# Third and fourth token group of a transformer block: x loaded by channels, its mean and scale sent through DRAM, in place of TensorE transposes

## The chip, the cores and the metric

The kernel runs on one core of a Trainium2 chip. A core has TensorE (in the profile PE for matmuls and PEld for the loads of weights), VectorE (DVE), ScalarE (ACT), GpSimd (POOL), and SyncE (SP), which here only issues transfers; 16 DMA engines move data between DRAM and the on-chip SBUF. Matmuls write to PSUM, of which the kernel holds eight banks of 128x512 numbers. Each engine works through its own instructions in order and waits by semaphores for the others. The metric is the device time of one execution in microseconds (us); the median of several runs counts.

## The reference

One transformer block over x, 2048 tokens of 1024 channels, all in 32-bit floats:

```python
x = x + _layernorm(attn(_layernorm(x), Wqkv, bqkv, Wo, bo))
x = x + _layernorm(ffn(_layernorm(x), W_gate, W_up, W_down))
# _layernorm(x) = (x - mean) / sqrt(var + 1e-5) over the channels
# attn: qkv = x @ Wqkv + bqkv, one head of 256; softmax(q k^T / 16) v; then @ Wo + bo
# ffn:  (silu(x @ W_gate.T) * (x @ W_up.T)) @ W_down.T, inner size 2752
```

The change touches the first `_layernorm(x)` and the form in which its result reaches the product with Wqkv.

## The kernel before

Each 32-bit factor of a matmul is kept as two parts, hi (a rounded copy, written by ScalarE) and lo (the source less hi, written by VectorE). The helper `split` (lines 108 to 110) makes both; line 109 is the copy, line 110 the subtraction. A product is then three matmuls (`mm3`, lines 140 to 144: hi hi, hi lo, lo hi) for each block of 128 channels.

A matmul contracts over the partitions, so the normalised x must lie with channels on the partitions: `xT[g]`, eight channel blocks x (hi, lo) x 512 tokens, for a group g of 512 tokens. There are four groups (NG = 4), each of four token tiles (TB = 4) of 128 tokens. `xT` has two buffers, used in turn: a tile of its own for groups 0 and 2, and `a2` for groups 1 and 3, so that the profile names the latter's writes "a". The rows of x come as token tiles, 128 tokens x 1024 channels, into four buffers `xin` = `f4[0:4]` (`load_x`, line 160, by SP's queue). For each tile:

- `norm_stats` (lines 112 to 122): two bn_stats over 512 channels (line 116), an aggregate (119) and the addition of epsilon (120) on VectorE, then the power -1/2 on GpSimd (121). Results are one mean and one scale per token, each a [128, 1] column of a small tile.
- the normalisation in place (line 127 in `norm_rows`; in the first two groups line 240 or 294 or, on ScalarE, 245).
- eight transposes of 128x128 on TensorE into two PSUM banks (line 135 in `transpose_rows`; line 251 in the first two groups), and hi and lo from the banks into `xT` (lines 109 and 110; 218 and 221 in the first two groups).

Groups 0 and 1 are prepared by code written out by hand (lines 292 to 354 and 467 to 482). Groups 2 and 3 are prepared in the loop of lines 483 to 490: in round g (1 to 3), step i of four calls `prep1((g + 1) * TB + i, ...)` (lines 164 to 170) for one token tile of the next group, and then `qk(g, i, ...)`, the i-th of four output blocks (k in two, q in two) of group g, 24 matmuls over the eight channel blocks into bank 4 or 5. After `prep1`, the buffer is loaded with the tile four further on. Then come the four `v_block(g, tb)`, 16 matmuls each into bank 6 or 7, one per token tile; such a block needs the eight channel blocks of its own 128 tokens alone. Drains of the banks: k by line 178 (ScalarE) and 179 (VectorE), q of groups 1 to 3 by line 182 and a store to DRAM (`q_d`, line 183), v by lines 193 to 195 with `split`. After the loop, `scores(0, j)` (lines 377 to 384; k of group j with q of group 0, six matmuls into bank j), the first softmax, and attention over 16 query tiles; then the gate, up and down products, which take most of the time.

The order of each engine's instructions is set by a scheduler that runs when the kernel is built and goes by priority (the order of the program) and by its own estimate of when data are ready. So PE's matmuls of one block can be mixed with those of another whose data are there. An instruction in `pin(...)` or with `tc.keep_in_program_order` stays behind the one traced just before it on its engine. The bn_stats of the loop are pinned in this way; line 127, the transposes of line 135, `split`, `qk` in the loop and `v_block` aren't.

Buffers that the change uses: `f2p[1]` and `f4[4]` (128 x 1024 each) hold raw weights in the first stage. After that `f4[4]` takes the q of the next group for attention (`q_load`, line 370, split by lines 374 and 375), `f4[0]` and `f4[1]` the rows of wo (line 512, on ScalarE's queue), and `f2p[1]`, `f4[1]` and `f4[3]` rows of x for the residual (line 1143).

Of the kernel before, what the change touches and what calls it, by code (L numbers as in the profile page):

```python
# [8 lines left out]
F32 = mybir.dt.float32  # L9
F32R = mybir.dt.float32r  # L10
AF = mybir.ActivationFunctionType
ALU = mybir.AluOpType
# [3 lines left out]
P = 128  # L16
T = 2048
C = 1024
D = 256
F = 2752  # L20
NT = T // P
NC_ = C // P
G = 512
NG = T // G
TB = G // P
# [6 lines left out]


@with_exitstack
def block_kernel(ctx, tc, x, wqk, wv, bqk, bv, wo, bo, wgu, wlast, wd, out):

# [9 lines left out]
    nc = tc.nc  # L48
# [4 lines left out]
    def tl(p, shape, dt, name):  # L53
        return p.tile(shape, dt, tag=name, name=name, bufs=1)
# [3 lines left out]
    ident = tl(cpool, [P, P], F32, "ident")  # L58
# [13 lines left out]
    def small_tile():  # L72
        small_n[0] += 1
        return small[small_n[0] % NSM]

    bank_pool = pool("banks", space=PSUM)
    bank = [tl(bank_pool, [P, 512], F32, f"bank{i}") for i in range(8)]

    dram = ctx.enter_context(tc.tile_pool(name="dram", bufs=1, space=bass.MemoryType.DRAM))
    q_d = [tl(dram, [P, 2, G], F32, f"q_d{g}") for g in range(NG)]  # L80
    xT_d = [tl(dram, [C, G], F32, f"xT_d{g}") for g in range(NG)]
    at_d = [tl(dram, [P, C], F32, f"at_d{t}") for t in range(NT)]
    x1_d = [tl(dram, [P, C], F32, f"x1_d{t}") for t in range(NT)]
# [10 lines left out]
    f4 = [tl(cpool, [P, C], F32, f"f4_{i}") for i in range(5)]  # L94
    f2p = [tl(cpool, [P, C], F32, f"f2p{i}") for i in range(2)]
# [9 lines left out]
    def f32(ap):  # L105
        return ap.bitcast(F32)

    def split(hi, lo, src, lo_engine=None):
        nc.scalar.copy(hi, src)  # L109
        (lo_engine or nc.vector).tensor_tensor(lo, src, f32(hi), ALU.subtract)  # L110

    def norm_stats(halves, pin=None):

        s = small_tile()
        for i, h in enumerate(halves):
            b = nc.vector.bn_stats(s[:, 6 * i : 6 * i + 6], h)
            if pin:
                pin(b)
        nc.vector.bn_aggr(s[:, 12:14], s[:, 0:12])
        nc.vector.tensor_scalar(s[:, 14:15], s[:, 13:14], EPS, None, ALU.add)  # L120
        nc.gpsimd.tensor_tensor(s[:, 15:16], s[:, 14:15], mhalf, ALU.pow)
        return s[:, 12:13], s[:, 15:16], s

    def norm_rows(t, pin):

        m, r, _ = norm_stats([t[:, 0:512], t[:, 512:1024]], pin)
        nc.vector.tensor_scalar(t, t, m, r, ALU.subtract, ALU.mult)

    def transpose_rows(t, dst, tb, banks):

        for hf in range(2):
            b = banks[hf]
            for j in range(4):
                cb = 4 * hf + j
                nc.tensor.transpose(b[:, j * P : (j + 1) * P], t[:, cb * P : (cb + 1) * P], ident)  # L135
            src = b.rearrange("p (j t) -> p j t", j=4)
            cols = slice(tb * P, (tb + 1) * P)
            split(dst[:, 4 * hf : 4 * hf + 4, 0, cols], dst[:, 4 * hf : 4 * hf + 4, 1, cols], src)

    def mm3(o, w, m, first, last, pin=lambda i: i):  # L140

        pin(nc.tensor.matmul(o, w[0], m[0], start=first, stop=False))  # L142
        pin(nc.tensor.matmul(o, w[0], m[1], start=False, stop=False))  # L143
        return pin(nc.tensor.matmul(o, w[1], m[0], start=False, stop=last))  # L144
# [6 lines left out]
    xin, wraw, qst = f4[0:4], [f4[4], f2p[1]], f2[0:2]  # L151
# [5 lines left out]
    xT = [tl(x0_pool, [P, 8, 2, G], F32R, "xT0"), a2]  # L157

    def load_x(t):
        nc.sync.dma_start(xin[t % TB], x[t * P : (t + 1) * P, :])  # L160

    WARM = 34

    def prep1(t, banks):

        r = xin[t % TB]
        norm_rows(r, tc.keep_in_program_order)
        transpose_rows(r, xT[(t // TB) % 2], t % TB, banks)
        if t + TB < NT:
            load_x(t + TB)  # L170

    def qk(g, i, b, pin=lambda i: i):
        xg = xT[g % 2]
        for c in range(8):
            mm3(b, (wqk_s[i][:, c, 0, :], wqk_s[i][:, c, 1, :]), (xg[:, c, 0, :], xg[:, c, 1, :]), c == 0, c == 7, pin)
        if i < 2 or g == 0:
            dst = kT(i, g) if i < 2 else qa[:, i - 2, :, :]
            pin(nc.scalar.activation(dst[:, 0, :], b, AF.Identity, bias=bqk_s[:, i : i + 1]))
            pin(nc.vector.scalar_tensor_tensor(dst[:, 1, :], b, bqk_s[:, i : i + 1], f32(dst[:, 0, :]), ALU.add, ALU.subtract))
        else:  # L180
            s = qst[i % 2]
            nc.scalar.activation(s, b, AF.Identity, bias=bqk_s[:, i : i + 1])
            nc.sync.dma_start(q_d[g][:, i - 2, :], s)

    def v_block(g, tb, b):
        xg = xT[g % 2]
        cols = slice(tb * P, (tb + 1) * P)
        for c in range(8):
            nc.tensor.matmul(b, xg[:, c, 0, cols], wv_s[:, c, :, :].rearrange("p a f -> p (a f)"), start=(c == 0), stop=False)  # L189
            nc.tensor.matmul(b[:, D:], xg[:, c, 1, cols], wv_s[:, c, 0, :], start=False, stop=(c == 7))  # L190
        k = g * TB + tb
        s = vst[tb % 2]
        nc.vector.tensor_tensor(s, b[:, :D], bv_s, ALU.add)
        nc.vector.tensor_tensor(s, b[:, D:], s, ALU.add)
        split(vt[:, k, 0, :], vt[:, k, 1, :], s)
# [4 lines left out]
    pin = tc.keep_in_program_order  # L200
# [33 lines left out]
    def stats(tb):  # L234
        r = xin[tb % TB]
        return norm_stats([r[:, L], r[:, R]], pin)
# [55 lines left out]
    m, r, _ = stats(0)  # L292
# [190 lines left out]
    for g in range(1, NG):  # L483
        for i in range(4):
            if g + 1 < NG:
                prep1((g + 1) * TB + i, (bank[2 * (i % 2)], bank[2 * (i % 2) + 1]))
            qk(g, i, bank[4 + i % 2])
        if 0 < g < NG - 1:
            for tb in range(TB):
                v_block(g, tb, bank[6 + tb % 2])  # L490
# [86 lines left out]
    pin = tc.keep_in_program_order  # L577
# [72 lines left out]
    class Slot:  # L650
        t = None
# [465 lines left out]
    for i in range(NT):  # L1117
# [40 lines left out]
        cb = i - EARLY - 3  # L1158
# [129 lines left out]
```

## Time and profile before

| what | value |
|---|---|
| median of 3 runs (lowest, highest) | 1676.95 us (1676.39, 1677.01) |
| profiled execution | 1676.83 us |
| its span in the trace | 1675.0 us |
| granted TensorE clock | 0.999 |
| DMA moved | 271.02 MB, mean 162 GB/s |

The span is the time from the first to the last instruction in the trace; 1.83 us of the profiled execution lie around it. An engine's busy time is the sum of its instructions' records. Matmuls are pipelined, so the record of one (386 ns for 512 columns) overlaps the next, and the distance between two starts is what one costs. "The chain" is the sequence of instructions and waits followed back from the last instruction: what isn't on it could be shorter at no effect. Views by line name the line of the kernel that issued an instruction; "a<-bank" means that tile a is written from a tile bank, buffer numbers left out. Transfers are listed by issue, with the time from the issue to the landing of the data.

### The profile page before, as it was taken

The numbers are of one execution on the slowest core, as the hardware profiler recorded it, in microseconds if no ns is written. First come the engines' busy times: TensorE is split into PE (matmuls) and PEld (weight loads), VectorE is DVE, ScalarE is ACT, GpSimd is POOL, SyncE is SP. The second block draws the span as 40 slices with busy tenths as digits, with TensorE's granted clock in tenths as the row PEclk, the third lists the DMA queues.
The fourth block names the chain that finished last, engine by engine and source line by source line (L and its number), as shares of the span: only waits on it lengthen the run. The fifth ranks groups of instructions, "written<-read, shape, count | busy, mean of one in ns | idle before, by whom it ended". The sixth has DMA issues, their size and how long they took to land.

```text
span 1675.0 us, 21258 instructions
## 1 busy us (share of the span) xinstructions
PE 1664.4 (99%) x7850; PEld 1391.1 (83%) x7850; DVE 1101.3 (66%) x1679; ACT 698.3 (42%) x1043; POOL 91.9 (5%) x121
## 2 busy tenths in 40 slices
PE   9999999999999999999999999999999999999998
PEld 8888888888888888888888888888888888888887
DVE  7553676767877777677578457965555665465458
ACT  4222455544634444444365444433333333354342
POOL 1000010000011111111000000100000000000001
PEclk9999999999999999999999999999999999999999
DMA  6221023335656666666468656533322223586653
GB/s 217 83 80 41 12 101 114 113 128 186 221 173 220 215 211 229 220 218 205 158 226 260 199 186 213 198 115 125 113 101 95 95 95 126 214 267 194 199 185 123
DMA packets 131160, 271.02 MB, mean 162 GB/s; under 512 B 13296, under 2 KB 30064, under 8 KB 131056
## 3 DMA queue, kind: packets, MB, share of 16 engines
q1 hardware_dynamic: 129616, 266.65, 47.7%
q10 hardware_dynamic: 1440, 3.02, 0.5%
q8 instruction: 61, 1.00, 0.3%
q14 instruction: 43, 0.35, 0.1%
HBM read 185.73 MB, written 83.89 MB: 161 GB/s over the span
## 4 chain that ended last, share of the span: by engine, by line
PE 96%; DVE 2%; DMA 1%; issue 0%; ACT 0%; POOL 0%; SPq 0%; POOLq 0%; DVEq 0%; ACTq 0%
PE bank L782 71%; PE bank L144 4%; PE bank L142 4%; PE bank L143 4%; PE bank L417 3%; PE bank L418 2%; PE bank L401 2%; PE bank L189 1%; PE bank L190 1%; PE bank L521 1%; PE bank L274 0%; PE bank L135 0%; DMA f<-x 0%; PE bank L968 0%; DMA out<-bo_s 0%
## 5 line engine op out<-in xcount | busy, mean ns | idle before, releaser
L782 PE MATMUL bank<-a 128*128 128x512 f32 (+1 forms) x960 | 226.4, 386 | 0.0
L782 PE MATMUL bank<-xb,a 128*128 128x512 f32 x912 | 212.5, 389 | 0.2 <-DVE a L110 0.2
L782 PEld LDWEIGHTS bank<-a 128*128 128x128 f32 x960 | 179.0, 188 | 36.6
L782 PEld LDWEIGHTS bank<-xb,a 128*128 128x128 f32 x912 | 170.9, 188 | 36.0 <-DVE a L110 0.6
L109 ACT CAST a<-f2p 128x1024 fp32r<-128x1024 f32 (+2 forms) x123 | 107.0, 870 | 115.1 <-PE bank L782 88.2
L110 DVE TENSOR_TENSOR a<-f2p,a 128x1024 fp32r<-128x1024 f32 (+2 forms) x123 | 122.4, 995 | 44.4 <-ACT a L109 40.4
L110 DVE TENSOR_TENSOR a<-f,a 128x1024 fp32r<-128x1024 f32 (+2 forms) x82 | 83.6, 1020 | 103.3 <-ACT a L109 101.3
L782 PE MATMUL bank<-kx,a 128*128 128x512 f32 x612 | 146.0, 389 | 0.0
L782 PE MATMUL bank<-a,a 128*128 128x512 f32 x588 | 139.7, 389 | 0.0
L782 PEld LDWEIGHTS bank<-kx,a 128*128 128x128 f32 x612 | 114.9, 188 | 23.8
L782 PEld LDWEIGHTS bank<-a,a 128*128 128x128 f32 x588 | 110.3, 188 | 23.0
L782 PE MATMUL bank<-wvo 128*128 128x512 f32 (+1 forms) x498 | 120.9, 386 | 0.0
L796 DVE TENSOR_TENSOR p_s<-bank,p_s 128x512 f32<-128x512 f32 x96 | 65.2, 682 | 81.7 <-PE bank L782 45.8
L109 ACT CAST a<-f 128x1024 fp32r<-128x1024 f32 (+2 forms) x82 | 62.6, 764 | 120.0 <-PE bank L782 98.6
L782 PEld LDWEIGHTS bank<-wvo 128*128 128x128 f32 x498 | 92.9, 188 | 18.9
L782 PE MATMUL bank<-a,wvo 128*128 128x512 f32 x444 | 106.0, 389 | 0.0
L782 PE MATMUL bank<-kx,wvo 128*128 128x512 f32 x420 | 100.1, 389 | 0.0
L782 PEld LDWEIGHTS bank<-a,wvo 128*128 128x128 f32 x444 | 83.3, 188 | 17.3
L782 PEld LDWEIGHTS bank<-kx,wvo 128*128 128x128 f32 x420 | 78.8, 188 | 16.4
L110 DVE TENSOR_TENSOR wvo<-f,wvo 128x1024 fp32r<-128x1024 f32 (+1 forms) x49 | 57.1, 1166 | 50.5 <-ACT wvo L109 50.5
L417 PE MATMUL bank<-a,a 128*128 128x512 f32 x240 | 89.4, 404 | 0.9 <-ACT f2p L523 0.6
L782 PE MATMUL bank<-kx 128*128 128x512 f32 (+1 forms) x339 | 78.5, 387 | 0.0
(285 smaller groups left out, 2908.4 us busy)
## 6 DMA issues: line engine op xcount, KB each, us to landing
f2p<-wgu SPq DMA_DIRECT2D x41, 512.0 KB, 5.4
f<-x SPq DMA_DIRECT2D x30, 512.0 KB, 3.8
hd_S<-p_s SPq DMA_DIRECT2D x60, 256.0 KB, 4.5
f<-wgu SPq DMA_DIRECT2D x22, 512.0 KB, 3.5
wr<-wgu SPq DMA_DIRECT2D x21, 512.0 KB, 5.6
f<-wd SPq DMA_DIRECT2D x20, 512.0 KB, 5.0
hd_A<-xi SPq DMA_DIRECT2D x40, 256.0 KB, 2.0
td_T<-f SPq DMA_DIRECT2D x40, 256.0 KB, 4.5
```

What stands on the lines that cost most here:

```text
L109: nc.scalar.copy(hi, src)
L110: (lo_engine or nc.vector).tensor_tensor(lo, src, f32(hi), ALU.subtract)
L142: pin(nc.tensor.matmul(o, w[0], m[0], start=first, stop=False))
L143: pin(nc.tensor.matmul(o, w[0], m[1], start=False, stop=False))
L144: return pin(nc.tensor.matmul(o, w[1], m[0], start=False, stop=last))
L189: nc.tensor.matmul(b, xg[:, c, 0, cols], wv_s[:, c, :, :].rearrange("p a f -> p (a f)"), start=(c == 0), stop=False)
L190: nc.tensor.matmul(b[:, D:], xg[:, c, 1, cols], wv_s[:, c, 0, :], start=False, stop=(c == 7))
L401: nc.tensor.transpose(b[:, n * P : (n + 1) * P], p_s[:, k * P : (k + 1) * P], ident)
L417: nc.tensor.matmul(b, p[:, k, 0, :], vt[:, k, :, :].rearrange("p h d -> p (h d)"), start=(k == 0), stop=False)
L418: nc.tensor.matmul(b[:, D:], p[:, k, 1, :], vt[:, k, 0, :], start=False, stop=(k == NKB - 1))
L782: one = nc.tensor.matmul(o, w[i], m[j], start=first and n == 0, stop=last and n == 2, skip_group_check=chained)
L796: nc.vector.tensor_tensor(o, a, b, op)
```

## The change

Groups 2 and 3 are prepared another way. A second input `xt` holds x of the last 1024 tokens transposed, as [2 groups, 1024 channels, 512 tokens], arranged on the host. In the first step of a round, the statistics of all four token tiles of the next group are taken from the rows, as before (`row_stats`). Mean and scale, eight [128, 1] columns, are stored to a DRAM tensor `mr_d` of [2, 512] by eight transfers; one transfer reads it back to all 128 partitions (`mr`, 1024 numbers per partition, 512 KB in all). Then four transfers load `xt` over the rows in the same four buffers, two channel blocks x 512 tokens in each (`load_columns`). In each of the four steps, `columns` subtracts the mean and multiplies by the scale, both with a different value for each column, repeated over the two channel blocks, and splits the result into `xT`. Then the buffer is loaded with the rows of the next group. The transposes of line 135, the banks 0 to 3 in the loop and the normalisation of line 127 are gone. Line numbers in the diff are those of its own.

```diff
@@ -78,6 +78,7 @@
     q_d = [tl(dram, [P, 2, G], F32, f"q_d{g}") for g in range(NG)]
+    mr_d = [tl(dram, [2, G], F32, f"mr_d{g}") for g in range(NG)]
@@ -161,13 +146,32 @@
-    def prep1(t, banks):
-
+    mr = {2: f2p[1], 3: f4[4]}
+
+    def row_stats(t):
         r = xin[t % TB]
-        norm_rows(r, tc.keep_in_program_order)
-        transpose_rows(r, xT[(t // TB) % 2], t % TB, banks)
-        if t + TB < NT:
-            load_x(t + TB)
+        m, rs, _ = norm_stats([r[:, 0:512], r[:, 512:1024]], tc.keep_in_program_order)
+        cols = slice((t % TB) * P, (t % TB + 1) * P)
+        for k, v in enumerate((m, rs)):
+            nc.sync.dma_start(mr_d[t // TB][k : k + 1, cols].rearrange("k p -> p k"), v)
+
+    def load_columns(g):
+        nc.sync.dma_start(mr[g].rearrange("p (k t) -> p k t", k=2), mr_d[g].partition_broadcast(P))
+        for n, r in enumerate(xin):
+            nc.sync.dma_start(r.rearrange("p (c t) -> p c t", c=2), xt[g - 2].rearrange("(n c p) t -> n p c t", c=2, p=P)[n])
+
+    def columns(g, n):
+
+        r = xin[n].rearrange("p (c t) -> p c t", c=2)
+        for k, op in enumerate((ALU.subtract, ALU.mult)):
+            v = mr[g][:, k * G : (k + 1) * G].unsqueeze(1).broadcast_to([P, 2, G])
+            nc.vector.tensor_tensor(r, r, v, op)
+        d = xT[g % 2][:, 2 * n : 2 * n + 2, :, :]
+        split(d[:, :, 0, :], d[:, :, 1, :], r)
+        if g + 1 < NG:
+            load_x((g + 1) * TB + n)
@@ -483,7 +487,11 @@
             if g + 1 < NG:
-                prep1((g + 1) * TB + i, (bank[2 * (i % 2)], bank[2 * (i % 2) + 1]))
+                if i == 0:
+                    for tb in range(TB):
+                        row_stats((g + 1) * TB + tb)
+                    load_columns(g + 1)
+                columns(g + 1, i)
             qk(g, i, bank[4 + i % 2])
@@ -1267,6 +1275,7 @@
+        "xt": x.reshape(2, 2 * G, C)[1].reshape(2, G, C).transpose(0, 2, 1),
```

Left out of the diff: the removal of `norm_rows` and `transpose_rows`, which nothing calls any more, and the parameter `xt` of the kernel.

## The prediction

> **What bounds the kernel now.** I read the busy shares first, then the chain that ended last, then the two stages that the change touches. On the page:
>
> ```profile
> span 1675.0 us, 21258 instructions
> PE 1664.4 (99%) x7850; PEld 1391.1 (83%) x7850; DVE 1101.3 (66%) x1679; ACT 698.3 (42%) x1043; POOL 91.9 (5%) x121
> ...
> PE 96%; DVE 2%; DMA 1%; issue 0%; ACT 0%; POOL 0%; SPq 0%; POOLq 0%; DVEq 0%; ACTq 0%
> ```
>
> TensorE is busy for 99% of the span and makes up 96% of the chain: time goes only where PE instructions go or where PE is made to wait. The changed loop (lines 483 to 490) runs from 56.85 us, when the first matmul of group 1 (counted from 0) starts, to about 131 us; group 2's first q/k matmul starts at 92.74 us. The view by stretches of time for its two rounds (columns: PE, PEld, DVE, ACT, POOL busy, granted clock, DMA share, GB/s):
>
> ```profile
> 56.85:92.74 35.89, 35.89 (x189) 30.55 (x188) 21.96 (x45) 8.97 (x16) 2.74 (x5) 1.00 0.27 88
> 92.74:130.90 38.16, 38.16 (x197) 32.19 (x196) 20.11 (x39) 9.12 (x16) 1.64 (x3) 1.00 0.25 84
> ```
>
> PE has no gap at a clock of 1.00. DVE is 61% and 53% busy, DMA a quarter: there is room beside PE, but not without end.
>
> **What is removed.** Eight token tiles with eight transposes each, 64 PE instructions. The chain view of 60 to 100 us prices a tile's eight:
>
> ```profile
> 66.22 0.87 PE bank L135 x8
> 71.68 0.87 PE bank L135 x8
> 79.38 0.87 PE bank L135 x8
> 88.90 0.87 PE bank L135 x8
> 97.48 0.87 PE bank L135 x8
> ```
>
> They stand on the chain, with matmuls directly before and after: 8 x 0.87 = **7.0 us**. (Their records sum to 8.28 us, because records overlap by the pipeline; the chain's figure is what the next matmul waits.) Per tile DVE loses one normalisation and two subtractions from PSUM, ACT two copies from PSUM. Rows: normalisation 0.81, subtractions 1.29 for the two, copies 1.07 for the two.
>
> **What is added.** Per channel tile: two 128x1024 tensor_tensor on DVE and one subtraction of that size, one ACT copy of 128x1024. The SBUF rows of that size say 1.22 us for DVE (line 221 at 28.02 us; neighbours follow after 1.14), 1.05 for ACT. A mean repeated over a middle dimension as second operand isn't in the trace; that row is the nearest and I take it, with the 0.81 us of the one-operand normalisation as the lower and 1.29 us as the upper end. DVE per tile: 3 x 1.14 = 3.4 us against 0.73 + 1.20 = 1.93 before; so +1.5 per tile, +6 per group. DVE goes to about 28 us in a round of PE that shrinks to some 33: 85%. ACT stays as it is. This is hidden as long as the order of arrival allows; so I follow the chain of each group.
>
> Group 2. The statistics now come in one block behind the last drain of group 0:
>
> ```profile
> 57.77 0.75 DVE L179 SCALAR_TENSOR_TENSOR qa<-bank,bqk_s,qa 128x512 fp32r<-128x512 f32 x1 [4.67 <-ACT qa L178]
> 58.44 1.28 DVE L116 BATCH_NORM_STATS2 small<-f 128x6 f32<-128x512 f32 x2
> 59.75 0.21 DVE L119 BATCH_NORM_AGGREGATE small<-small 128x2 f32<-128x12 f32 x1
> 60.00 0.15 DVE L120 TENSOR_SCALAR small<-small 128x1 f32<-128x1 f32 x1
> ```
>
> 58.44 to 60.15 is 1.71 us a tile, four end at 65.3; all four x tiles were issued by 51.6 us, and bn_stats is pinned behind the DVE instruction traced before it, which here is the previous tile's line 120. POOL's power (0.55) ends at 65.9. Then eight stores of [128,1] go by SP's queue, 0.33 us of issue each (up to 0.48, the row of bqk_s); six are out before, in a stretch where that queue has no other issue until 67 us. Store, wait and load by DRAM exist for q:
>
> ```profile
> 82.83 0.33 SPq L183 DMA_DIRECT2D q_d<-f2p  x1
> 85.68 0.33 SPq L370 DMA_DIRECT2D f<-q_d  x1
> ```
>
> 2.85 us from a store's issue to that of its reader, which SP had waited for. The mean/scale load is 512 KB, like the x loads of 4.2 us (list of DMA issues, below). So 66.0 + 2.85 + 4.1 = **73 us**. Bounds for both from that list (KB each, us to landing):
>
> ```profile
> f<-x SPq DMA_DIRECT2D x17, 512.0 KB, 4.2
> ...
> q_d<-f2p SPq DMA_DIRECT2D x4, 256.0 KB, 2.0
> ...
> f2p<-x SPq DMA_DIRECT2D x1, 512.0 KB, 3.4
> ...
> bo_s<-bo SPq DMA_DIRECT2D x1, 512.0 KB, 9.6
> ...
> bqk_s<-bqk SPq DMA_DIRECT2D x1, 2.0 KB, 9.0
> ```
>
> The small pieces of bqk_s (16 bytes in each partition) and the broadcast bo_s took 9.0 and 9.6 us, but at 4 to 5 us of the span, behind some 3 MB of loads. At 73 us only the four column loads (2 MB) stand in the queues, free to go from 60 us as each tile's statistics have read it. So I take the uncrowded rows and keep 12 us of lateness (9.0 + 0.3 + 9.6 against 2.85 + 4.1) as the upper end per group; the lower end is 1 us early.
>
> First pair of channel blocks: 73 + 2 x 1.14 + 1.05 + 1.2 = 77.5. The others follow by 3.4, with 3.2 us of other DVE work between (one k drain 0.75, two v blocks of 1.25): the last at **91 us**. PE: v_block of group 2 starts at 86.27 behind three tiles' transposes, so group 1's own work would end at 86.27 - 3 x 0.87 = 83.7. Then PE has scores(0,0) and scores(0,1) (banks 0 and 1 are now free): 12 matmuls of 0.228, 2.7 us. Each ready pair gives qk of two banks, 12 x 0.228, and two v blocks' share, 4 x 0.35: 4.1 us against 3.4 that DVE needs for the next. Pairs 0 to 2 (77.5, 81, 87) carry PE to 83.7 + 2.7 + 12.3 = 98.7, beyond 91. If the matmuls go in a stricter order (one qk alone, 1.37 us per pair), pair 3 is wanted at 83.7 + 2.7 + 4.1 = 90.5: at most 1, without the scores 3 us late. What goes away here is v_block of group 2 as a filler: by token tiles two of its blocks ran before group 2's tiles were complete; by channels all wait for the last pair.
>
> Group 3. load_x of tile 12 + n must now wait until pair n is split, the last at 91, landing at 95; statistics end at 96.7, POOL 97.3, store and reader 100.2, landing 104.2, pairs at 109, 112, 116 and, with the drains, 122. PE's own work of group 2 (96 x 0.228 + 64 x 0.176 = 33.1) ends at 83.7 + 33.1 = 116.8, three score blocks fill to 120.9, pairs 0 to 2 are there. Nothing to 1 us. SP issues eight stores, one load and four column loads more per group (13 x 0.33 = 4.3 us of 33); behind them wait q's stores, whose buffers are wanted a round later. The q load into f4[4] and wo's loads into f4[0], f4[1] slip by some 30 and 15 us: in the trace of before q_split runs at 123 and wo's splits at 162, later than their new landings at about 126 or close to it, and q of group 1 is wanted four attention tiles on.
>
> Sum: 1676.83 (the profiled execution: span 1675.0 and 1.83 around it) - 7.0 + stall of 0 to 3.3, of which I take 0.5 = 1670.3; the median of the runs is 0.1 above the profiled one: **1670.4**.
>
> **Two rules against the change.** The Trainium skill, "DMA: Bandwidth & Descriptors", "Rules for kernel authors", wants many small transfers made one large, since under 64 KB one pays mostly overhead, and its "Specifications" see a read-modify-write below 512 bytes; the 16 stores here move 4 bytes per partition. Its fixed part of about 2.0 us ("Anatomy of one DMA", for the GpSimd path) would, as an estimate, be 16 us if eight were paid in turn, and the sum would be like that of the slower rival. No run here yet shows such a store.
>
> **Rivals.** (1) *The new chain is late by some microseconds.* For it: DVE at 85% and in order, four transfers in line where none was. Against: PE's fillers, and that no PE wait between 25 and 131 us shows in before. Stall 3.3 to 10, time 1673.6 to 1680.3, say 1676: no difference. (2) *Slower: DRAM round trips that take the place of the transposes.* Each us by which store and broadcast land later than 73 moves pair 3 of group 2, and group 3 twice, as its x loads hang on group 2's pairs. With strict order the stall is about e in group 2 and e - 3 in group 3 for a lateness e: 2e - 3, so break-even at e = 5, slower by over 0.2% from e = 6.7. At the upper end, e = 12: 21 us, +14, 1691; with interleaved matmuls about 12.5, 1682; say 1686. For it only the crowded rows speak. (3) *It doesn't do what it says*, PE's 7 us return as waits in the softmax stage: before has only 1.4 us of PE idle from 160 to 300 us, and nothing there loses slack; up to 1676.8.
>
> **Chances and range.** Forecast (up to 1673.5) 0.62, all faster. Rivals 1 and 3: 0.18, same, which here means within 0.2% (3.35 us), about what a measurement of this kernel can tell from no change. Rival 2: 0.20, slower. Low end: 7.0 plus the 1.4 of idle gone, 1668.5. High end: to leave out at most 2 in 10 it takes in rivals 1 and 3 and part of rival 2: 1684. The forecast's own range is 1669.8 to 1673.5.
>
> **What would show it.** Right: no line 135; PE busy down by about 8 us of records; PE gapless from 57 to 120; the mean/scale load landing near 73 us, its store taking 2 to 3; group 2's first q/k matmul by 87. Wrong: PE waiting on DVE's xT near 84 to 95 or 117 to 130, stores of 5 us and more, DVE held at the first subtraction of the mean, drains of lines 179 or 193 behind it.

## The result, and the profile after

The changed kernel took 1704.22 us (median of 6 runs, 1698.78 to 1706.46) against 1676.98 for the kernel before: a ratio of 1.016, with a 95% interval of 1.0145 to 1.0175. It is slower by 27 us; the prediction had 1670.4, at most 1684. The profiled execution took 1705.52 us, 28.7 more than that of before.

The page of the changed kernel, span, busy times and the chain by engine:

```profile
span 1703.4 us, 21178 instructions
PE 1661.0 (98%) x7786; PEld 1385.9 (81%) x7786; DVE 1110.6 (65%) x1679; ACT 698.0 (41%) x1035; POOL 92.1 (5%) x121
...
PE 92%; DMA 4%; DVE 2%; issue 1%; ACT 0%; POOL 0%; POOLq 0%; DVEq 0%; SPq 0%
```

The 64 transposes are gone (7850 - 7786), and PE has less to do than before. But 4% of the chain are now transfers. The view by stretches of time of the changed kernel says where:

```profile
56.85:92.74 35.89, 26.95 (x125) 22.18 (x123) 11.03 (x22) 2.76 (x4) 2.20 (x4) 0.92 0.58 80
92.74:131.00 38.26, 31.29 (x137) 25.67 (x137) 21.27 (x35) 7.55 (x10) 2.20 (x4) 0.90 0.59 131
131.00:170.00 39.00, 23.97 (x101) 19.83 (x102) 22.17 (x29) 8.51 (x12) 0.00 (x0) 0.74 0.35 108
```

PE, full before, is idle for 9, 7 and 15 us, at a granted clock of 0.92, 0.90 and 0.74. In the first stretch the DMA engines are busy for 58% of the time and move only 80 GB/s; before it was 27% for 88. The waits of PE from 55 to 180 us are two, one ahead of each group (us in total, times, longest; line 127 is the first matmul of a q/k product in the changed kernel):

```profile
PE bank L127 <- ACT a L110: 17.7, 1, 17.7
PE bank L127 <- ACT xT L110: 13.2, 1, 13.2
```

What the hi copies of line 110 waited for, in the chain of 55 to 180 us (start, us, what):

```profile
61.40 12.20 DMA f<-xt
...
73.67 11.89 DMA mr_d<-small
...
85.60 4.47 DMA f2p<-mr_d
...
90.09 4.70 DVE f L170 x5
```

The last small store (`mr_d<-small`) was issued at 73.67, because SP had first waited for the load of an xt tile to land, from which the store needs nothing (why, is said under "Stores alone"); it took 11.9 us more until the load of mean and scale could be issued. That load took 4.5, near the predicted 4.1. SP's timeline shows the pause ahead of the last stores:

```profile
64.14 1.20 SPq L158 DMA_DIRECT2D mr_d<-small  x2
70.39 0.38 SPq L163 DMA_DIRECT2D f<-xt  x1
70.86 3.12 SPq L158 DMA_DIRECT2D mr_d<-small  x2
85.60 0.32 SPq L161 DMA_DIRECT2D f2p<-mr_d  x1
```

The list of DMA issues (KB each, us to landing) shows that both the 512-byte stores and the 512 KB loads beside them were slow:

```profile
f<-xt SPq DMA_DIRECT2D x8, 512.0 KB, 13.2
...
mr_d<-small SPq DMA_DIRECT2D x16, 0.5 KB, 13.1
```

The waits are 30.9 us. PE's timeline around the first one:

```profile
83.52 0.28 PE L194 MATMUL bank<-wvo,a 128*128 128x256 f32 x1
97.04 0.80 PE L127 MATMUL bank<-xT,wqk 128*128 128x512 f32 x1 [13.24 <-ACT xT L110]
97.63 0.63 PE L127 MATMUL bank<-kx,qa 128*128 128x512 f32 x1
```

The clock fell to half during each wait and stayed there for a while after it: from 97.04 to 100.49 us and from 146.03 to 151.64 us the trace has 8 and 13 matmul distances of which most are 0.43 us, in place of 0.23; that is 3.45 - 1.84 and 5.61 - 2.99, together an estimated 4.2 us. -7.0 + 30.9 + 4.2 = 28.1 of the 28.7.

### The profile page after: what moved, and what is told of

Its sections match the earlier page's. It is cut to its first block, busy times and chain, and to the rows that moved or that the text cites. A ratio compares the mean times of both kernels' runs of the same rounds, so it can differ in the third digit from the quotient of the medians.

```text
span 1703.4 us, 21178 instructions
## 1 busy us (share of the span) xinstructions
PE 1661.0 (98%) x7786; PEld 1385.9 (81%) x7786; DVE 1110.6 (65%) x1679; ACT 698.0 (41%) x1035; POOL 92.1 (5%) x121
## 4 chain that ended last, share of the span: by engine, by line
PE 92%; DMA 4%; DVE 2%; issue 1%; ACT 0%; POOL 0%; POOLq 0%; DVEq 0%; SPq 0%
PE bank L790 71%; PE bank L127 3%; PE bank L128 3%; PE bank L129 3%; PE bank L421 3%; DMA f<-xt 2%; PE bank L422 2%; PE bank L405 2%; DMA mr_d<-small 1%; PE bank L193 1%; DVE f L170 1%; PE bank L529 1%; DMA f<-x 1%; DVE small L117 1%; PE bank L194 0%
## 5 line engine op out<-in xcount | busy, mean ns | idle before, releaser
L111 DVE TENSOR_TENSOR a<-f,a 128x1024 fp32r<-128x1024 f32 (+2 forms) x86 | 88.3, 1028 | 106.5 <-ACT a L110 104.2
L110 ACT CAST a<-f 128x1024 fp32r<-128x1024 f32 (+2 forms) x86 | 66.7, 776 | 152.2 <-PE bank L790 99.1
```

## The experiments

Theory A: stores in pieces of 4 bytes are slow by themselves and hold up what shares the DMA engines. Rival B: they are slow only because the xt loads stand in the same queues. Rival C: SP's queue can have only so many transfers under way. Each profile below is that of one execution.

**No wait for the stores.** Mean and scale come from a row of x; the stores still run.

```diff
-        nc.sync.dma_start(mr[g].rearrange("p (k t) -> p k t", k=2), mr_d[g].partition_broadcast(P))
+        nc.sync.dma_start(mr[g], x[g, :].partition_broadcast(P))
```

> The changed kernel, but mean and scale of groups 2 and 3 are loaded from a row of x, so that nothing waits for the 16 small stores, which still run (the normalisation of these two groups is thus with other numbers). Theory A (pieces of 4 bytes are slow by themselves and hold up whatever shares the DMA engines): the PE waits of 13 and 18 us before groups 2 and 3 go, but xt loads still take 10 us and more to land beside the stores; 1670 to 1676. Theory B (stores and loads are only slow because 2 MB of xt loads stand in the same queues): the same here, xt loads 5 to 13 us, 1670 to 1674. If it stays above 1690, the wait for the round trip by DRAM isn't the cause.

1692.64 us, a miss for both theories: with the round trip gone, more than half of the loss stayed. The list of DMA issues from 55 to 170 us and the waits of PE of this run:

```profile
f<-xt SPq DMA_DIRECT2D x8, 512.0 KB, 11.0
```

```profile
PE bank L127 <- DVE kx L183: 14.2, 2, 8.4
```

The xt loads take 11 us beside the stores, VectorE waits for them with its subtractions, and the drain of a k block (line 183) stands behind these in its queue; PE waits for the drain's bank.

**No stores at all.** The same, with `row_stats` ending after the statistics.

```diff
-        for k, v in enumerate((m, rs)):
-            nc.sync.dma_start(mr_d[t // TB][k : k + 1, cols].rearrange("k p -> p k"), v)
```

> As the run without a wait, and the 16 stores are left out as well. A: with no pieces of 4 bytes the xt loads land in 4 to 6 us in place of a median of 13.2; about 1670. B: the xt loads crowd each other and stay near 10 us; about 1670 too. The landing time of the xt loads tells them apart, not the total.

1669.62 us, 7.00 below the kernel before (1676.62 in these runs). The xt loads from 55 to 170 us:

```profile
f<-xt SPq DMA_DIRECT2D x8, 512.0 KB, 3.9
```

Issued 1.6 us and more apart, as here, the loads hardly crowd each other: 3.9 us with no stores beside them, 13.2 with them. All that the change loses hangs on 16 stores of 512 bytes and on the wait for them.

**Stores alone.** The xt loads are pinned behind the load of mean and scale on SP's queue.

```diff
-            nc.sync.dma_start(r.rearrange("p (c t) -> p c t", c=2), xt[g - 2].rearrange("(n c p) t -> n p c t", c=2, p=P)[n])
+            tc.keep_in_program_order(nc.sync.dma_start(r.rearrange("p (c t) -> p c t", c=2), xt[g - 2].rearrange("(n c p) t -> n p c t", c=2, p=P)[n]))
```

> The changed kernel with the four xt loads of a group held on SP's queue behind the load of mean and scale, so that the eight stores run alone. A: the stores still take 8 us and more, the round trip stays at 12 us or so, and the xt loads come 4 us later on top: 1704 to 1714. B: the stores land in 2 to 3 us, mean and scale by 74 us, xt by 80: 1671 to 1680. A limit on the transfers in flight on SP's queue (C) would also give the latter, as only eight are under way.

1685.15 us. The median landing of the stores of both groups:

```profile
mr_d<-small SPq DMA_DIRECT2D x16, 0.5 KB, 7.5
```

With next to nothing else under way the stores still take 7.5 us, so neither B nor C is why a store is slow: the eighth, issued at 66.5 without a wait for a landing, has landed by 74.2, when the load of mean and scale goes out. The xt loads, now 0.5 us apart behind that load and with no store beside them, took 6.8 to 8.7 us in group 2: so close together, loads do crowd each other.

But C's limit exists, and it had a part in the changed kernel. In none of the 15 traces of this case does SP have more than eight transfers under way. In the changed kernel five issues (70.39, 73.67, 119.44, 120.03 and 126.80 us) follow within 0.07 us on the landing of the transfer eight places before them (70.33, 73.60, 119.38, 119.97, 126.73). By this the last store went at 73.67 and 126.80 us, though the power that it stores had ended at 66.6 and 114.5. It is slow landings that fill the eight places: in the runs below with as many stores per group that land fast, no issue waited in this way. So the limit adds to what a slow store costs; how much of the total is its share was not tested.

The total is 19 us better than the changed kernel's, which A had not expected: slow stores beside loads cost more than slow stores and then loads, and the last store of group 2 goes 7 us earlier.

**One store of 32-byte pieces.** The statistics of four tiles are collected in one [128, 8] tile `a`, mean and scale of each tile side by side.

```diff
+        nc.vector.bn_aggr(a[:, 2 * tb : 2 * tb + 2], s[:, 0:12])
...
+        if tb == TB - 1:
+            nc.sync.dma_start(mr_d[t // TB], a[:, 0:8])
...
+            v = mr[g].rearrange("p (t b k) -> p k b t", b=TB, k=2)[:, k, :, :]
```

> The changed kernel with mean and scale of four tiles in one [128, 8] tile and one store of it per group, 128 pieces of 32 bytes, in place of eight stores with 1024 pieces of 4 bytes; read back to all partitions as before (512 KB) and used with a stride of 8 numbers, in four tensor_tensor of 512 columns per pair. A: an eighth of the pieces, landing in 2 to 4 us, mean and scale at about 73 to 75 us, no long PE wait: 1670 to 1676. B: the store still stands behind xt loads, some 8 to 10 us: 1685 to 1700. C: only 6 transfers per group instead of 13, so nothing waits for an issue: 1670 to 1676.

1688.43 us, ratio 1.0069 (1.0052 to 1.0085). The store landed in 3.2 us beside the xt loads, which took 4.2, and mean and scale were there at 73.6 us: the prediction's 73. The time was lost behind that, in VectorE's timeline of this run:

```profile
73.64 17.07 DVE L180 TENSOR_TENSOR f<-f,f2p 128x512 f32<-128x512 f32 x16 [3.31 <-DMA f2p<-mr_d]
```

16 instructions of 512 columns at 1.07 us, where half of a contiguous one of 1024 columns is 0.57: the operand read with a stride of 8 numbers nearly doubles the price. And all 16 come before the first subtraction of a split (at 90.63 us), so that the first pair was complete only when the last nearly was. This order was in the changed kernel too.

**PSUM in place of DRAM**, and the same with VectorE's order mended.

```diff
+            b = bank[2 * (t // TB % 2) + k]
+            nc.tensor.transpose(b[:, cols], v.broadcast_to([P, P]), ident)
...
+            v = bank[2 * (g % 2) + k].unsqueeze(1).broadcast_to([P, 2, G])
```

```diff
+            with tc.issue_after(last_tt[0].ins) if n + k else nullcontext():
+                last_tt[0] = nc.vector.tensor_tensor(r, r, v, op)
```

> The changed kernel without DRAM for mean and scale: per tile two TensorE transposes of the [128, 1] columns repeated over 128 columns, which put the mean and the scale of 512 tokens into two PSUM banks for all partitions; VectorE reads them there. 16 transposes of about 0.11 us come back (1.8 us) of the 7.0 us that the 64 took. If the small stores and the round trip are the whole cause, no long PE wait is left and the time is 1676.9 - 7.0 + 1.8 = 1671.8, up to 1674 if the order of VectorE (all subtractions and multiplications before the first hi/lo split) costs some. If that order is a cause of its own weight, 1676 and more.

> As the run with PSUM in place of DRAM, and on VectorE each pair's subtraction queued behind the multiplication of the pair before, so that splits can start pair by pair. 1671.8, and below the run without this order by what that order costs (0 to 3 us).

1671.66 us (ratio 0.9971, 0.996 to 0.9982) and 1671.69 (0.997, 0.9959 to 0.9982): faster than before by 5 us, as expected. The order makes no difference here, since the first subtraction starts at 70.5 us and PE wants the first pair after 83:

```profile
70.53 9.13 DVE L170 TENSOR_TENSOR f<-f,bank 128x1024 f32<-128x1024 f32 x8
```

**The order alone**, in the changed kernel.

> The changed kernel with this order on VectorE alone, stores as they are. The first hi part came 3.4 us later than it would have pair by pair, before both groups: the PE waits of 13 and 18 us should be some 3.4 us shorter each, 1697 to 1700. If the order plays no part, 1704.

1698.59 us, one run; the changed kernel's six runs go from 1698.8 to 1706.5, so the total alone doesn't show it. The trace does: mean and scale landed, PE went on 3.7 us after the first subtraction started (87.4 to 91.1), against 7.0 (90.1 to 97.0) in the changed kernel; 2.75 us came back at once as a wait for the lo part.

**PE kept busy in the waits**, to price the half clock.

```diff
+            if g > 1 and i == 0:
+                for _ in range((0, 0, 110, 140)[g]):
+                    pin(nc.tensor.transpose(bank[3][:, 0:P], ident, ident))
```

> The changed kernel with 110 and 140 idle transposes of the identity (0.11 us each, 12 and 15 us) before the first q/k block of groups 2 and 3, in the time in which PE waits; the rest is as it is. If the half clock after the waits is a cost of its own, some 20 matmuls at 0.43 in place of 0.23 us are back at 0.23: 4 to 5 us less than the changed kernel, 1699 to 1701, with a granted clock of 1.00 after the waits. If not, 1704 or more.

1731.78 us, a miss. Only the first 110 stood in a wait (83.5 to 95.7 us); the 140 ran after the second one. And the new schedule put a k drain on VectorE behind subtractions that waited for mean and scale, so that PE waited 24.9 us for it. What the run does show is the clock of the first wait, by stretches of 10 us (granted clock in the third column from the end):

```profile
80.00:90.00 10.00, 10.00 (x82) 9.54 (x81) 0.73 (x1) 0.00 (x0) 0.00 (x0) 1.00 0.39 80
90.00:100.00 10.00, 6.51 (x54) 5.97 (x53) 10.00 (x10) 4.66 (x5) 0.00 (x0) 0.95 0.05 10
```

In the changed kernel the clock was half from 86.7 us on; under the transposes it stayed full, and fell near 99, after PE had idled for most of 95.7 to 99.6. So idle transposes keep the clock up, but the price of the half clock in the total is only read off the matmul distances, not tested.

**Width and place of the pieces**, with the stores alone as above: 128 pieces of 32 bytes, 256 bytes apart; 128 pieces of 4 bytes, 512 apart; 128 pieces of 4 bytes, 4 x DIST apart (DIST is 8 and 16 for groups 2 and 3 in one run, 2 and 4 in the next).

```diff
+    mr_d = [tl(dram, [P, 8, 8], F32, f"mr_d{g}") for g in range(NG)]
...
+    nc.sync.dma_start(mr_d[t // TB][:, 2 * (t % TB) + k, :], small_of[0][:, 8:16])
```

```diff
+    mr_d = [tl(dram, [P, 8, 16], F32, f"mr_d{g}") for g in range(NG)]
...
+    nc.sync.dma_start(mr_d[t // TB][:, 2 * (t % TB) + k, 0:1], v)
```

```diff
+    mr_d = [tl(dram, [8, P, DIST.get(g, 2)], F32, f"mr_d{g}") for g in range(NG)]
...
+    nc.sync.dma_start(mr_d[t // TB][2 * (t % TB) + k, :, 0:1], v)
```

> As the run with the stores alone (eight stores of 128 pieces of 4 bytes landed 7.5 us after issue in the median, the last after 7.6), but each of the eight stores writes 128 pieces of 32 bytes, each to a place of its own, 256 bytes from the next piece of the same store; what is read back is not the mean and scale, so the normalisation of groups 2 and 3 uses other numbers. If the number of pieces sets the time: 7 us again. If the width of 4 bytes, or several engines' writes to one short stretch of DRAM, sets it: 2 to 3.5 us, as one store of 32-byte pieces took 3.2.

> As the run with the stores alone, with the same 4-byte pieces, but each piece lies 512 bytes from the next in DRAM in place of 4 (what is read back is not the mean and scale, so the normalisation of groups 2 and 3 uses other numbers). If neighbouring 4-byte writes hinder each other: landing in 2 to 4 us. If a 4-byte write is slow wherever it goes: 7 us again.

> The stores alone, 4-byte pieces 32 bytes apart in DRAM for group 2 and 64 bytes apart for group 3 (4 bytes apart: 7.4 us in the median; 512 bytes apart: 1.4). A small load of the pieces comes behind them; mean and scale are taken from a row of x, so the normalisation of groups 2 and 3 uses other numbers. If pieces hinder each other only where they share a stretch of 32 bytes, both groups land in 1.4 us; with 64 bytes, group 2 lands in between and group 3 in 1.4; if only the distance in 512 bytes counts, both stay near 7.

> As the run with 32 and 64 bytes, with 8 bytes (group 2) and 16 bytes (group 3) between the starts of 4-byte pieces. If pieces within one stretch of 32 or 64 bytes are written one behind the other, the time of a store falls with the number of pieces that share the stretch: some 4 to 6 us at 8 bytes, 2 to 4 at 16. If the cause is only that pieces touch each other, both land in 1.4.

Totals: 1671.26, 1676.63, 1670.78 and 1671.01 us. The eight stores of a group in the list of DMA issues, for 32-byte pieces; for 4-byte pieces 32 bytes apart; for 8 bytes; and for 16 bytes:

```profile
mr_d<-small SPq DMA_DIRECT2D x8, 4.0 KB, 1.4
```

```profile
mr_d<-small SPq DMA_DIRECT2D x8, 0.5 KB, 1.4
```

```profile
mr_d<-small SPq DMA_DIRECT2D x8, 0.5 KB, 2.9
```

```profile
mr_d<-small SPq DMA_DIRECT2D x8, 0.5 KB, 1.9
```

| distance of 4-byte pieces in DRAM | 4 | 8 | 16 | 32 | 64 | 512 bytes |
|---|---|---|---|---|---|---|
| pieces per 32 bytes | 8 | 4 | 2 | 1 | 1 | 1 |
| median landing, us | 7.4, 8.3 | 2.9 | 1.9 | 1.4 | 1.4 | 1.4 |

So theory A falls in its form: neither the 4 bytes nor the 128 pieces are slow. Slow is that several pieces go to the same 32 bytes of DRAM. As soon as each piece has a stretch of 32 bytes of its own, a store lands in 1.4 us. The step is clear from 8 bytes (single stores took 2.6 to 3.2 us) to 32; at 16 bytes they took 1.4 to 3.3. Both medians are below what was expected for them. How the writes hinder each other is not seen in the trace. In the run with 512 bytes the stores landed as fast as with 32 and 64, PE had no long wait up to 170 us, but it idled 3.4 us from 170 to 300 and 2.6 from 300 to 900 (1.4 and 0.1 in the run with 32 and 64); that kernel has two transfers more at its start, and its later stages are scheduled otherwise. What made it 6 us slower was not tried.

**One store, put in order by ScalarE.** From these: one store of 32-byte pieces, read back as it lies, two ScalarE copies of 128x512 that undo the interleaving, and the mended order.

```diff
+        w = f4[4].rearrange("p (t b k) -> p k b t", b=TB, k=2)
+        for k in range(2):
+            nc.scalar.copy(mr[g][:, k * G : (k + 1) * G].rearrange("p (b t) -> p b t", b=TB), w[:, k, :, :])
```

> The changed kernel with one store of the [128, 8] tile per group (as in the run with one store), the read-back put in order once by two ScalarE copies of 128x512, so that VectorE reads mean and scale without a stride, and the pairs ordered on VectorE. If few pieces that are not 4 bytes wide are the whole cure: mean and scale at 74 us as in that run, in order at 76, pairs from 80 on, no PE transposes come back: 1669.7 to 1671, that is 1 to 2 us below the version by PSUM. If the read-back itself is too late for the first pairs, PE waits of 1 to 5 us: 1671 to 1676.

1670.93 us (1670.13 to 1671.07), ratio 0.9965, interval 0.9952 to 0.9979: faster than both kernels, by 5.6 and 33 us. It isn't to be told from the version by PSUM, whose interval overlaps. VectorE starts as soon as the copies are done, pair by pair:

```profile
75.16 3.69 DVE L184 TENSOR_TENSOR f<-f,f2p 128x1024 f32<-128x1024 f32 x3 [4.90 <-ACT f2p L172]
78.83 1.23 DVE L112 TENSOR_TENSOR xT<-f,xT 128x1024 fp32r<-128x1024 f32 x1
```

## Why the prediction was wrong, step by step

- **What is removed: right.** 8 x 0.87 = 7.0 us. Without the stores the kernel was 7.00 us faster (one run).
- **VectorE's added work: right in size, wrong in order.** The subtraction with a repeated mean took 1.22 us, the row it was priced by. But the prediction had the pairs one after the other, the first hi copy 2.3 us after mean and scale. The schedule made all four subtractions before the first multiplication, so PE went on 7.0 us after the landing. Nothing in the rows of before spoke for pair by pair; it was assumed.
- **Store, wait and load by DRAM: the step that failed.** "2.85 us from a store's issue to that of its reader" was the row of a 256 KB store of q, whose 2 KB pieces lie apart. The small stores had 11.9 and 7.9 us from the last issue to the reader's, with a median landing of 13.1. The upper end of 12 us of lateness came from loads that queued, and was too low: mean and scale landed at 90.1 in place of 73, 17 us late. Of these, 7.7 came before the last issue (73.67 in place of 66.0), 9.1 from there to the reader's issue (11.9 in place of 2.85) and 0.4 in the load. No row of before held a store of small pieces side by side; an estimate from rows of other kinds was called a bound.
- **The xt loads: wrong by the same cause.** The row of 4.2 us was right for loads without the stores (3.9); beside the stores they took 13.2. That a slow store takes the loads beside it along was in no rival. Nor was it foreseen that SP would issue xt loads between the stores and, with eight transfers under way, wait for one of them to land: "six are out before" held, but the last store went at 73.67, not 66.
- **Slack of PE: right; its fillers: wrong.** With mean and scale read back by 73.9 us and the mean in order at 75.2 (one store, put in order), PE had no long wait before either group, as the working had it for 73. But the 12 score matmuls that the working put ahead of group 2, 2.7 us, did not run there: in the changed kernel the first of them (`bank<-kx,qa`) stood at 97.63, behind the first q/k matmul that waited, and before group 3 none ran either. So nothing shortened the two waits.
- **The rivals.** Rival 2 had the mechanism and the sign, at 0.2. Its formula for a strict order, 2e - 3, gives 31 us at e = 17, and the waits were 30.9. That is luck: by group it gives 17 and 14, the waits were 13.2 and 17.7; in group 2 PE waited for the first pair, where the rival has pair 3; and VectorE's order is in the waits and not in the formula. Its price ended at 1691, since e ended at 12, and since it had no term for the clock. The ends of rival 1, 1673.6 and 1680.3, add its stall to 1670.3, which already holds 0.5.
- **The clock: left out.** 4.2 us by the matmul distances.
- **The two rules.** The Trainium skill's "DMA: Bandwidth & Descriptors", "Rules for kernel authors", pointed the right way: one store in place of eight landed in 3.2 us; but eight stores of pieces 32 bytes apart landed in 1.4 each, so it isn't the number of stores. Its "Specifications" put the penalty below 512 bytes; here pieces of 32 bytes, and of 4 bytes 32 bytes apart, landed in 1.4 us, and only pieces within the same 32 bytes were slow. The page speaks of the rate, the runs of the time to landing; for the latter the measurement decides.

## What to carry to other kernels

A [128, 1] column that is to lie in a row of DRAM is 128 writes of 4 bytes side by side: collect several columns so that each partition writes at least 32 bytes, or turn the column with TensorE, and don't price such a store by the landing time of a large one. A long wait that TensorE never had before costs, as here with 13 and 18 us, the wait and then a while at half clock. Where a chain is replaced by one that a scheduler orders, ask for the order of the first result: here all subtractions came before the first product that PE could use.

## What the runs showed of the hardware

- Stores of 4-byte pieces to DRAM, eight of 128 pieces one behind the other: 7.4 to 8.3 us to landing at a distance of 4 bytes, 2.9 at 8, 1.9 at 16 (single ones 1.4 to 3.3), 1.4 from 32 bytes on. Beside 512 KB loads the slow ones took 13.1 and the loads 13.2 in place of 3.9.
- SP never had more than eight transfers under way, in any trace here; with eight, the next issue waited for a landing (73.67 us after 73.60, 126.80 after 126.73). Whether the chip or the program sets this limit is not shown.
- TensorE's clock went to half some 3 us after PE's last matmul (83.5 and 128.1 us; half from 86.7 and 131.0) and back 3.3 and 5.5 us after it went on. The half stretches lasted 13.65 and 20.48 us, four and six times 3.41, and the full one between them 30.72, nine times. That agrees with the Trainium skill, "TensorE: Matmul & The Clock Gate", "Part 1: The HAM clock gate", which tells of a free-running window of 3413 ns. Its budget for the work at half clock is about one window; here it was 0.96 and 1.6 windows, so it can be more than one.
- A VectorE operand read with a stride of 8 numbers: 1.07 us for 512 columns, against 0.57, half of a contiguous one of 1024.
- A transpose of a column repeated over 128 columns puts it on all partitions in PSUM. 16 of these cost 2.0 us in the totals (1671.66 against 1669.62, one run, without them and without the stores).
